# Conv, scan and attention hybrid on one core: B spread by one bf16 product, later sums, and other stages placed by estimates

## The chip, the cores and the metric

The kernel runs on one core of a Trainium2 chip. The metric is device time in microseconds (us) of one execution. The kernel before takes 9288.97 us (median of three runs, 9285.59 to 9299.49). Engines are called as the profile calls them: PE is TensorE (PEld its weight loads), DVE is VectorE, ACT is ScalarE, POOL is GpSimd, SP is SyncE.

## The reference, cut to what matters

Four images of 56 x 56 tokens and 96 channels pass two layers with a selective scan, each in four directions, then two attention and feed-forward layers. The heart is this recurrence over 3136 tokens, for 192 channels with 16 states each:

```python
def step(h, inp):
    da_t, db_t, x_t, c_t = inp
    h = da_t * h + db_t * x_t[..., None]
    y_t = jnp.einsum('bds,bs->bd', h, c_t)
    return (h, y_t)
...
dt = jax.nn.softplus(jnp.einsum('blr,dr->bld', dt_raw, dtw) + dtb)
d_a = jnp.exp(dt[..., None] * a)
d_b = dt[..., None] * b_ssm[:, :, None, :]
```

Two layers, four images and four directions, cut in chunks of 448 tokens, make 224 chunks. A chunk has eight rounds of three scans over 128 lanes: 1792 rounds, 5376 scans.

## The kernel before

One round spreads B over 128 lanes (TensorE, an fp32 product with a selection matrix), multiplies it with dt times u into `v` (VectorE, the third of three products often GpSimd), scans (VectorE, with the decays of ScalarE in PSUM), multiplies with C into `hc` (GpSimd), and sums over the states (TensorE).

```python
def begin(n):
    ch, e, q = rounds[n]
    b = self.spread_b(ch, q)                       # PE: sel x cf, fp32
    v = sp.tile([128, NG, CS + 2], F32, name="v", bufs=3)
    ahead = NQ * e + q not in (OWN_TAIL if ch.l and ch.i else OWN)
    if ahead:                                      # third product on GpSimd
        nc.gpsimd.tensor_tensor(v[:, 2, TOKENS], ch.du[e][:, 2], ch.cb[q][:, 1], ALU.mult)
    return b, v, ahead
...
for n, (ch, e, q) in enumerate(rounds):
    b, v, ahead = nxt
    for g in range(2 if ahead else 3):
        nc.vector.tensor_tensor(v[:, g, TOKENS], ch.du[e][:, g], b, ALU.mult)
    nxt = begin(n + 1)
    self.prepare(ch, nexts.get(ch), r)             # the next chunk's cf, dt, du
    yield "C", n, r                                # gap for other stages
    for g in range(NG):
        if g == 2:
            yield "F", n, r                        # second gap
        nc.vector.tensor_tensor_scan(v[:, g, way], da[g][:, way], v[:, g, way], 0.0, ALU.mult, ALU.add)
        ...
        decay(n + 1, g)                            # ACT: exp into da[g]
        if g == 1:
            carried(n + 1, nxt[1])                 # ACT: carried state into v
    hc = ...                                       # POOL: v times C
    if late is not None:
        self.add_up(*late)                         # PE: sums of round n - 1
    late = (ch, e, q, hc)
```

The other stages (loading, the middle with its convolution, the tails) are generators. At each `yield` of the scans they proceed by one step, thinned by fixed turns:

```python
if slot == "F":
    next(rest, None)
elif (r != 2 or p > 4) and taken * FULL <= TURNS[p] * u:
    taken += 1
    next(rest, None)
...
alone(net.tail(3))                                 # the last image's tail, after the scans
```

A stretch below is one layer and image, 28 chunks. Beside stretch 0 runs the loading, beside 1 to 4 the middles of images 0 to 3, beside 5 to 7 the tails of images 0 to 2.

Of the kernel before, what the change touches and what calls it, by code (L numbers as in the profile page):

```python
# [20 lines left out]
HS = 56  # L21
# [15 lines left out]
NW = 13  # L37
NWIN = 3
OWN = (3, 4, 5)
OWN_TAIL = (4, 5)  # L40

FULL = 4 * NCS * NE * NQ - 13
TURNS = (150, 150, 150, 150, 150, 220, 220, 220)
BANKS = 2
DEPTH = 3
ORDER = ((0, 0), (0, 1), (1, 0), (1, 1))
WD = NE * 128 + C + NE + NE * NQ * NG
# [32 lines left out]
def lay_out(i):  # L80
# [28 lines left out]
    for l, (xw, dw, db, al, dd) in enumerate(scan):  # L109
        r = RANK[l]  # L110
        for k in range(4):
            t = xw[k].T
            m = np.zeros((128, NE, 2, 64), np.float32)
            m[:C, :, 0, :32] = np.concatenate([t[:, r + NS :], t[:, r : r + NS]], 1).reshape(NE, C, 32).swapaxes(0, 1)
            m[:C, :, 0, 32 : 32 + r] = t[:, :r].reshape(NE, C, r).swapaxes(0, 1)
            m[:, :, 1] = m[:, :, 0]
            wt = np.zeros((128, C), np.float32)
            for e in range(NE):
                wt[64 * e + 32 : 64 * e + 32 + r] = dw[k].T[:, C * e : C * e + C]
            bias = np.zeros((128, NE), np.float32)  # L120
            bias[:C] = db[k].reshape(NE, C).T
            a = al[k].reshape(NE, NG, 32, 4, NQ).transpose(3, 2, 0, 4, 1).reshape(128, -1)
            wd[l, k] = np.concatenate([m.reshape(128, -1), wt, bias, a], 1)
        c128.add(f"{l}D", dd.T.reshape(NE, C, 4).swapaxes(0, 1))
# [35 lines left out]
class Net:  # L160
    def __init__(self, ctx, tc, aps, at, out):
# [5 lines left out]
        self.dram = pool("dram", bufs=1, space=bass.MemoryType.DRAM)  # L167
        self.setup()
        self.dg = None
        self.held = self.lend = 0  # L170
        self.U = [self.big.tile([C, L], F32, name=f"U{e}") for e in range(NE)]
        self.Y = [self.big.tile([C, L], F32, name=f"Y{e}") for e in range(NE)]
        self.sp = pool("scan", bufs=2)
        self.wp = pool("work", bufs=2)
        d = lambda name, *shape: [self.dram.tile(list(shape), F32, name=f"{name}{i}") for i in range(NB)]
        self.xd, self.xrd = d("x", C, L), d("xr", C, L)
        self.ud, self.zd, self.yd, self.md = d("u", DI, L), d("z", DI, L), d("y", DI, L), d("m", DI, L)

    def ps(self):
        return self.psum.tile([128, 512], F32, tag="ps", name="ps", bufs=BANKS)  # L180

    def w(self, rows=128):
        return self.wp.tile([128, CW], F32, tag="w", name="w", bufs=NW)[:rows]
# [42 lines left out]
    def setup(self):  # L226
# [17 lines left out]

        self.sel = const.tile([128, NQ, 128], F32, name="sel")
        for q in range(NQ):
            nc.vector.tensor_copy(
                self.sel[:, q].rearrange("p (s d) -> p s d", s=4),
                self.ident[:, NS + q : NS + q + 13 : 4].unsqueeze(2).to_broadcast([128, 4, 32]),
            )  # L250
# [78 lines left out]
        with tc.tile_pool(name="stage", bufs=1) as st:  # L329
            t = st.tile([C, 2, 3, 128], F32, name="q96")  # L330
# [75 lines left out]
    def parameters(self, ch):  # L406

        nc, sp = self.nc, self.sp
        if ch.first:
            for n in range(4):  # L410
                a = slice(n * L // 4, (n + 1) * L // 4)
                for e in range(NE):
                    nc.sync.dma_start(self.U[e][:, a], self.ud[ch.i][C * e : C * e + C, a])
        if ch.step == 0:
# [5 lines left out]
            p.wt = wd[:, a : a + C]  # L420
            a += C
# [4 lines left out]
        ch.par = self.p  # L426

# [19 lines left out]
    def step_size(self, ch, e, ps):  # L447
        rows = slice(64 * e + 32, 64 * e + 32 + RANK[ch.l])
        self.nc.tensor.matmul(ps[:C], ch.par.wt[rows], ch.cf[rows], start=True, stop=True)
# [46 lines left out]
    def prepare(self, ch, follow, r):  # L496
# [9 lines left out]
        elif r == 1:  # L506
            self.step_sizes(follow)
        elif r == 2:
            self.softplus(follow)
        elif r == 3:  # L510
# [13 lines left out]
    def prepare_ahead(self, far, r):  # L524

        if far is not None:
            if r == 5:
                self.parameters(far)
            elif r > 5:
                self.project_step(far, r - 6)  # L530

    def spread_b(self, ch, q):

        ps = self.psum.tile([128, 512], F32, tag="b", name="b", bufs=1)[:, :CS]
        self.nc.tensor.matmul(ps, self.sel[:, q], ch.cf, start=True, stop=True)  # L535
        return ps

    def scans(self):
# [9 lines left out]
        for l in range(2):  # L548
            for i in range(NB):
                for n, (orient, rev) in enumerate(ORDER):  # L550
                    for step in range(NCS):
# [4 lines left out]
                        ch.first = n == 0 and step == 0  # L556
# [7 lines left out]
        self.parameters(first)  # L564
        self.project_step(first, 0)
# [20 lines left out]
        def begin(n):  # L586
# [4 lines left out]
            if ahead:  # L591
                nc.gpsimd.tensor_tensor(v[:, 2, TOKENS], ch.du[e][:, 2], ch.cb[q][:, 1], ALU.mult)  # L592
            return b, v, ahead

        def carried(n, v):
            ch, e, q = rounds[n]
            at = CS + 1 if ch.rev else 0
            if ch.step:
                nc.scalar.copy(v[:, :, at : at + 1], ch.par.carry[:, e, q].unsqueeze(2))  # L599
# [4 lines left out]
        late = None  # L604
        for n, (ch, e, q) in enumerate(rounds):
# [8 lines left out]
            if more:  # L614
                nxt = begin(n + 1)
            self.prepare(ch, nexts.get(ch), r)
            yield "C", n, r
            self.prepare_ahead(afters.get(ch), r)
            if late is not None and late[2] == 0 and n > 1:
                self.keep_sums(*rounds[n - 2])  # L620
            for g in range(NG):
                if g == 2:
                    yield "F", n, r
# [7 lines left out]
                if more:  # L631
                    decay(n + 1, g)
                    if g == 1:
                        carried(n + 1, nxt[1])
            hc = sp.tile([128, NG, CS], F32, name="hc")
            nc.gpsimd.tensor_tensor(hc, v[:, :, TOKENS], ch.cb[q][:, 0].unsqueeze(1).to_broadcast([128, NG, CS]), ALU.mult)  # L636
            if late is not None:
                self.add_up(*late)
            late = (ch, e, q, hc)
        self.add_up(*late)  # L640
# [3 lines left out]
    def add_up(self, ch, e, q, hc):  # L644

        nc = self.nc
        if q == 0:
            self.y = self.psum.tile([128, 512], F32, tag="y", name="y", bufs=1)[:, :CS]

        for n, g in enumerate((0, 1, 2, 2)):  # L650
            nc.tensor.matmul(  # L651
                self.y[32 * n : 32 * n + 32], self.four, hc[:, g], start=q == 0 or n == 3, stop=n == 3,
            )
        if q < NQ - 1:
            return
        o = self.y[:C].rearrange("p (a b) -> p a b", b=HS)
        a, w = (self.U[e], self.skip[ch.l][:, e]) if ch.skip else (self.Y[e], self.ident[:C, :C])
        nc.tensor.matmul(o, w, self.in_order(a, ch.orient, ch.c * CS, CS), start=False, stop=True)  # L658

    def keep_sums(self, ch, e, q):  # L660
# [3 lines left out]
        if ch.last:  # L664
            self.nc.sync.dma_start(self.yd[ch.i][C * e : C * e + C], self.Y[e])
# [17 lines left out]
    def spread_factor(self, eps, *terms):  # L683
# [10 lines left out]
        yield "F0"  # L694
# [3 lines left out]
        yield "C1"  # L698
# [7 lines left out]
    def normed(self, eps, x, held, out=None):  # L706

        xc = self.factor(x)
        yield "F0"
        sq = self.squares(xc)  # L710
        yield "C1"
# [6 lines left out]
    def project(self, l, i, xr, s):  # L718
# [4 lines left out]
        yield "C2"  # L723
# [4 lines left out]
        yield "C1"  # L728
        t = [self.w(), self.w()]
        nc.scalar.activation(t[0], ps[0], AF.Silu, bias=b[:, 1:2])  # L730
        nc.scalar.activation(t[1][64:], ps[1][64:], AF.Silu, bias=b[64:, 2:3])
        nc.scalar.activation(t[1][:64], ps[1][:64], AF.Identity, bias=b[:64, 2:3])
        p = self.ps()[:, :CW]
        nc.tensor.matmul(p, self.in_w[l][:, :128], xr, start=True, stop=True)
        yield "F0"
# [27 lines left out]
    def conv(self, diag, win, lo, *parts):  # L763
# [5 lines left out]
        for n, tap in enumerate(taps):  # L769
# [9 lines left out]
            if n % 2 and n < 8:  # L779
                yield "C1"  # L780
# [10 lines left out]
    def overlap(self, part, n, depth):  # L791

        live, c = [], 0
        while live or c < n:
            if self.slot == "C" and c < n and len(live) < depth:
                live.append([part(c), "C0", 0])
                c += 1
            for g in list(live):
                new = int(g[1][1:])
                if g[1][0] == self.slot and sum(h[2] for h in live) - g[2] + new <= BANKS - self.lend:  # L800
# [3 lines left out]
            self.held = sum(h[2] for h in live)  # L804
            yield


    def load(self, i):
# [3 lines left out]
        def part(c):  # L812
# [4 lines left out]
            yield "C1"  # L817
# [3 lines left out]
            yield "F0"  # L821
            x = self.w(C)
            nc.scalar.copy(x, ps)
            yield "C1"
# [4 lines left out]
        yield from self.overlap(part, NCW, DEPTH)  # L829

    def middle(self, i):
# [5 lines left out]
        def part(c):  # L837
# [8 lines left out]
            yield "C1"  # L846
# [3 lines left out]
            yield "C1"  # L850
# [4 lines left out]
            yield "C0"  # L855
            g.append(self.w())
            nc.scalar.activation(g[0], ps[0], AF.Gelu, bias=self.b1[:, :1])
            yield "C2"
# [3 lines left out]
            yield "C0"  # L862
# [3 lines left out]
            yield "C1"  # L866
# [3 lines left out]
            yield "C1"  # L870
# [5 lines left out]
        yield from self.overlap(part, NCW, DEPTH)  # L876

        if self.dg is None:
            yield from self.run(self.diagonals(par("c128", "1conv_wa"), par("c128", "1conv_wb")[:64]))
            self.dg = self.got  # L880
        dga, dgb = self.dg

        def convolve(c):
# [4 lines left out]
            yield "C1"  # L888
            ps = self.ps()[:, :CW]
            yield from self.conv(dga, wa, lo, (ps, c * CR, CR))  # L890
            yield "C1"
            t = self.w()
            nc.scalar.activation(t, ps, AF.Silu, bias=par("c128", "1conv_ba"))  # L893
            ps = self.ps()
# [3 lines left out]
            yield "C0"  # L898
# [8 lines left out]
        yield from self.overlap(convolve, NCW, 2)  # L907

    def run(self, part):

        def whole(_):
            yield "C1"
            self.got = yield from part

        yield from self.overlap(whole, 1, 1)


    def tail(self, i):
# [3 lines left out]
        if len(self.dg) > 1:  # L922
            yield from self.run(self.diagonals(par("c96", "1dw_w")))
            self.dg = self.got
        (dgx,) = self.dg

        def part(c):
# [5 lines left out]
            yield "C1"  # L933
# [3 lines left out]
            yield "F0"  # L937
            fo = self.w(C)
            nc.scalar.activation(fo, ps, AF.Relu, bias=self.bn1[1], scale=self.bn1[0])
            yield "C1"  # L940
# [4 lines left out]
            yield "F0"  # L945
            nc.scalar.activation(fo, ps, AF.Identity, bias=self.bf)
            yield "C1"
# [3 lines left out]
            yield "F1"  # L951
            sa = self.squares(pa)
            yield "C1"
# [4 lines left out]
            yield "F1"  # L958
            nc.scalar.activation(yb, pb, AF.Square)
            yield "C1"  # L960
            nc.vector.tensor_tensor(zb, zb, pb, ALU.mult)
            f = yield from self.spread_factor(1e-5, (sa, self.avg192), (yb, self.avg192[:64]))
            yield "F0"
            rs = self.w(C)
            nc.scalar.copy(rs, f)
            yield "C1"
# [3 lines left out]
            yield "C1"  # L970
            nc.vector.tensor_tensor(rs, rs, ps, ALU.mult)
            xc = self.factor(fo, rs)
            yield "F0"
            sq = self.squares(xc)
            nc.scalar.activation(fo, xc, AF.Copy, scale=par("c96", "1fus_ln_g"))
            yield "C1"
# [7 lines left out]
            yield "F0"  # L984
            nc.scalar.activation(x, x, AF.Identity, bias=par("c96", "1fus_ln_b"))
            yield "C1"
# [4 lines left out]
        yield from self.overlap(part, NCW, DEPTH)  # L991
        for n in range(2):
            yield from self.run(self.attention(n))
            wq, bq = self.got

            def ffn(c):
# [4 lines left out]
                yield "C1"  # L1001
                ps = self.ps()[:C, :CW]
                nc.tensor.matmul(ps, wq, xr, start=True, stop=True)
                yield "C1"
                nc.vector.scalar_tensor_tensor(x, ps, bq, x, ALU.add, ALU.add)
                xc = self.factor(x)
                yield "F0"
# [3 lines left out]
                yield "C1"  # L1011
                f = yield from self.spread_factor(1e-5, (sq, self.avg96[:, :1]))
                yield "C1"
                xq = self.wp.tile([C, CW], F8, name="xq", bufs=DEPTH)
                nc.vector.tensor_tensor(xq, xs, f, ALU.mult, saturate=False)
                h = self.wp.tile([128, 3, CW], F16, name="h", bufs=2)
                ps = self.ps()[:, :CW]
                nc.tensor.matmul(ps, self.w1q[:, n, 0, :], xq, start=True, stop=True)
                yield "F0"
                nc.scalar.copy(h[:, 0], ps)  # L1020
                nc.scalar.activation(h[:, 0], h[:, 0], AF.Relu, bias=self.b1q[:, n, :1])
                yield "C2"
# [4 lines left out]
                yield "F0"  # L1027
# [3 lines left out]
                yield "C1"  # L1031
                hq = self.wp.tile([128, 3, CW], F8, name="hq", bufs=2)
# [150 lines left out]
```

## Time and profile before

| | before |
|---|---|
| start to first scan | 121 us |
| scans | 8675 us |
| tail after the scans | 507 us |
| busy in the scans: VectorE, GpSimd, TensorE | 7881, 7338, 7172 us |
| VectorE idle in the scans | 8675 - 7881 = 794 us |

The length of a stretch or a round in this document is the distance between the starts of its first scan and of the next one's, in the timeline of VectorE. The prediction shows the views that carry its argument. Two lines of the page that it does not show matter later: the clock granted to TensorE in forty slices (tenths of full speed), and the group of the sums (count, busy us, mean ns of one, idle time before and its releaser).

```profile
PEclk8988899888888888888898889888898889988875
L651 PE MATMUL y<-hc,four 128*32 128x448 f32 x14336 | 1980.0, 628 | 424.5 <-POOL hc L636 396.2
```

The clock stands at eight or nine tenths through the scans.

### The profile page before, as it was taken

To read this page: it belongs to the slowest core of one execution; us is meant where nothing else is said; L and a number is where in the kernel's file an instruction comes from. 1 tells how busy PE (TensorE), PEld (TensorE's weight loads), DVE (VectorE), ACT (ScalarE), POOL (GpSimd) and SP (SyncE) were. 2 spreads that over 40 slices of the span, in tenths; PEclk is the share of its full clock that TensorE was granted. 3 is DMA by queue.
4 is the path that set the end of the run, shared out by engine and by line. 5 is a ranking of instruction groups with operands and counts; after the bars stand their busy time and mean duration, and the time that the engine had idled before them with its cause. 6 is when DMAs were issued, how large, how long until landed. Compare 5 with 4: busy or idle time off the path is not lost.

```text
span 9302.9 us, 112892 instructions
## 1 busy us (share of the span) xinstructions
PE 7648.6 (82%) x30134; PEld 2655.7 (29%) x30134; DVE 7967.6 (86%) x10251; ACT 6080.1 (65%) x12093; POOL 7416.2 (80%) x3872
## 2 busy tenths in 40 slices
PE   7788787787878778887878879888898879988786
PEld 3222122222222222221222223332332223332244
DVE  5999999988998989989898989999889998999711
ACT  5777677666776667666776656666666666666523
POOL 4889888878887888878887888888888888888711
PEclk8988899888888888888898889888898889988875
DMA  5777766656666676667666676656666666666411
GB/s 154 177 177 169 172 169 162 155 138 170 168 157 147 157 172 164 155 148 172 166 162 149 154 180 154 149 148 150 176 152 155 150 154 162 157 154 153 115 33 31
DMA packets 940551, 1415.81 MB, mean 152 GB/s; under 512 B 175042, under 2 KB 926148, under 8 KB 938276
## 3 DMA queue, kind: packets, MB, share of 16 engines
q1 hardware_dynamic: 939136, 1406.79, 62.0%
q8 instruction: 238, 3.90, 0.2%
q14 instruction: 405, 3.32, 0.1%
q10 hardware_dynamic: 772, 1.80, 0.1%
HBM read 1139.85 MB, written 268.14 MB: 151 GB/s over the span
## 4 chain that ended last, share of the span: by engine, by line
PE 31%; DVE 25%; issue 12%; ACT 12%; DMA 10%; POOL 6%; SPq 3%; DVEq 0%; POOLq 0%; ACTq 0%
DVE v L626 17%; DVE v L612 7%; PE b L535 6%; PE y L651 5%; PE ps L775 4%; POOL hc L636 4%; ACT da L584 4%; DMA cb<-cd 3%; PE y L658 3%; PE pp L401 2%; DMA du<-dd 2%; PE ps L693 2%; PE ps L701 1%; SPq L485 1%; ACT L584 1%
## 5 line engine op out<-in xcount | busy, mean ns | idle before, releaser
L636 POOL TENSOR_TENSOR hc<-v,cb 128x1344 f32<-128x1344 f32 x1792 | 5155.8, 2877 | 1033.1 <-DVE v L626 571.3
L626 DVE TENSOR_TENSOR_SCAN v<-da,v 128x449 f32<-128x449 f32 (+1 forms) x5376 | 5469.6, 1071 | 362.8 <-ACT v L599 298.2
L584 ACT ACTIVATE da<-dt,na 128x448 f32<-128x448 f32 x5376 | 3358.5, 634 | 1531.4 <-DVE v L626 1477.4
L535 PE MATMUL b<-cf,sel 128*128 128x448 f32 x3584 | 2062.6, 661 | 804.5 <-DVE v L612 794.2
L612 DVE TENSOR_TENSOR v<-du,b 128x448 f32<-128x448 f32 x4172 | 2332.5, 606 | 297.3 <-PE b L535 275.0
L651 PE MATMUL y<-hc,four 128*32 128x448 f32 x14336 | 1980.0, 628 | 424.5 <-POOL hc L636 396.2
L592 POOL TENSOR_TENSOR v<-du,cb 128x448 f32<-128x448 f32 x1204 | 1378.5, 1145 | 81.1 <-DMA cb<-cd 64.9
L535 PEld LDWEIGHTS b<-cf,sel 128*128 128x128 f32 x3584 | 636.8, 212 | 2406.3 <-DVE v L612 1793.5
L651 PEld LDWEIGHTS y<-hc,four 128*32 128x32 f32 x14336 | 298.6, 114 | 1856.3 <-POOL hc L636 1104.8
L697 POOL TENSOR_TENSOR rs<-rs,power 112x4 f32<-112x4 f32 x252 | 254.3, 1010 | 685.2 <-ACT rs L696 498.5
L663 ACT COPY Y<-y 96x448 f32<-96x448 f32 x448 | 340.7, 761 | 623.8 <-PE y L658 623.0
L401 PE MATMUL pp<-U,wd 96*128 96x448 f32 x896 | 645.0, 807 | 75.1 <-DMA wd<-in_wd_dram 69.8
L775 PE MATMUL ps<-win,dg 64*64 64x220 f32 (+11 forms) x2016 | 567.3, 479 | 31.2 <-ACT w L893 30.7
L468 POOL TENSOR_TENSOR duc<-dtc,U 96x448 f32<-96x448 f32 x448 | 562.7, 1256 | 11.6 <-ACT dtc L462 11.6
L658 PE MATMUL y<-Y,ident 96*96 96x448 f32 x672 | 546.6, 902 | 0.0
L584 ACT ACT_TABLE_LOAD x385 | 494.0, 1283 | 14.4 <-DMA dt<-dd 7.5
L630 ACT COPY carry<-v 128x3 f32<-128x3 f32 x1536 | 293.6, 191 | 127.2 <-DVE v L626 123.9
L693 PEld LDWEIGHTS ps<-avg,w 96*112 96x112 f32 (+1 forms) x2240 | 315.2, 208 | 126.1 <-issue 53.2
L775 PEld LDWEIGHTS ps<-win,dg 64*64 64x64 f32 (+2 forms) x2016 | 249.6, 166 | 324.0 <-issue 255.3
L701 PE MATMUL ps<-ident,rs 112*96 112x112 f32 x2016 | 301.6, 307 | 33.3 <-POOL rs L697 31.1
L701 PEld LDWEIGHTS ps<-ident,rs 112*96 112x96 f32 x2016 | 281.5, 203 | 156.4 <-issue 77.2
L693 PE MATMUL ps<-avg,w 96*112 96x1 f32 (+1 forms) x2240 | 308.5, 255 | 20.0 <-ACT w L680 5.1
(218 smaller groups left out, 5497.3 us busy)
## 6 DMA issues: line engine op xcount, KB each, us to landing
cb<-cd SPq DMA_DIRECT2D x3584, 112.0 KB, 4.0
dt<-dd SPq DMA_DIRECT2D x1792, 168.0 KB, 4.0
du<-dd SPq DMA_DIRECT2D x1792, 168.0 KB, 3.7
dd<-dtc SPq DMA_DIRECT2D x448, 168.0 KB, 2.0
dd<-duc SPq DMA_DIRECT2D x448, 168.0 KB, 2.0
U<-u SPq DMA_DIRECT2D x64, 294.0 KB, 6.9
y<-Y SPq DMA_DIRECT2D x16, 1176.0 KB, 6.7
z<-w SPq DMA_DIRECT2D x56, 224.0 KB, 2.4
```

The costliest lines, as they stand in the source:

```text
L401: self.nc.tensor.matmul(ch.ps.rearrange("p (a b) -> p a b", b=HS), ch.par.wx[:, e], self.in_order(self.U[e], ch.orient, ch.c * CS, CS), st ...
L535: self.nc.tensor.matmul(ps, self.sel[:, q], ch.cf, start=True, stop=True)
L584: nc.scalar.activation(da[g][:, TOKENS], ch.dt[e][:, g], AF.Exp, scale=ch.par.na[:, e, q, g : g + 1])
L592: nc.gpsimd.tensor_tensor(v[:, 2, TOKENS], ch.du[e][:, 2], ch.cb[q][:, 1], ALU.mult)
L612: nc.vector.tensor_tensor(v[:, g, TOKENS], ch.du[e][:, g], b, ALU.mult)
L626: nc.vector.tensor_tensor_scan(v[:, g, way], da[g][:, way], v[:, g, way], 0.0, ALU.mult, ALU.add)
L636: nc.gpsimd.tensor_tensor(hc, v[:, :, TOKENS], ch.cb[q][:, 0].unsqueeze(1).to_broadcast([128, NG, CS]), ALU.mult)
L651: nc.tensor.matmul(self.y[32 * n : 32 * n + 32], self.four, hc[:, g], start=q == 0 or n == 3, stop=n == 3,)
L658: nc.tensor.matmul(o, w, self.in_order(a, ch.orient, ch.c * CS, CS), start=False, stop=True)
L693: nc.tensor.matmul(ps[:NT, q : q + 1], sq[:, b], avg, start=n == 0, stop=n == len(terms) - 1)
L701: nc.tensor.matmul(ps[:, b], rs[:, q : q + 1].to_broadcast([NT, C]), self.ident[:NT, :NT], start=True, stop=True)
L775: self.nc.tensor.matmul(o[:, a - r0 : e - r0, x0:x1], diag[:, tap], win[:, a + dy - lo : e + dy - lo, x0 + dx : x1 + dx], start=n == 0, st ...
```

## The change

The intent: TensorE gets rid of the four passes of fp32 for B, nothing that VectorE waits for stands behind GpSimd or behind other stages, and other stages are placed by what ScalarE and TensorE have to spare. B is kept exact: the projection writes B three times into `cf`, GpSimd subtracts the upper 16 bits once and twice, and one bf16 product adds the three upper halves.

```diff
-        self.nc.tensor.matmul(ps, self.sel[:, q], ch.cf, start=True, stop=True)
+        self.nc.tensor.matmul(ps, self.sel[:, q], self.upper(ch.cf), start=True, stop=True)
+    def upper(self, x):
+        return x.bitcast(BF16).rearrange("p (t h) -> p t h", h=2)[:, :, 1]
+    def split(self, ch, n):
+        x = ch.cf[64 + 32 * n :]
+        self.nc.gpsimd.tensor_tensor(x, x, self.upper(x), ALU.subtract)
...
-OWN = (3, 4, 5)
-OWN_TAIL = (4, 5)
+OWN = (3, 4)
+OWN_TAIL = (3,)
+SPARE = (1.2, 3.0)
+ACT_LIMIT, PE_LIMIT = 4.3, 6.0
...
             more = n + 1 < len(rounds)
             if more:
-                nxt = begin(n + 1)
+                nxt = begin(n + 1)                 # now copies the carried state too
+            if len(late) == 2:
+                ended = late.pop(0)
+                self.add_up(*ended)                # sums of round n - 2, after B
             self.prepare(ch, nexts.get(ch), r)
+            self.half_round()
+            self.spend((0.6, 0, 3.8, 0, 0, 0, 0, 0)[r], ...)
+            self.limit = ACT_LIMIT if r >= SOFTPLUS else 0.5 + 0.95 * 2 * (SOFTPLUS - r)
             yield "C", n, r
...
+    def half_round(self):
+        self.backlog = [max(0.0, a - b) for a, b in zip(self.backlog, SPARE)]
+    def room(self, act, pe):
+        a, p = self.backlog
+        return not self.paced or (act == 0 or a + act <= self.limit) and (pe == 0 or p + pe <= PE_LIMIT)
...
-            yield "C1"
+            yield "C0 a3.2"                        # a step's estimate: 3.2 us of ScalarE
...
+                if p == 7:
+                    lanes.insert(0, chain(net.fuse(3), net.attend(3)))
+    net.late()                                     # eight banks, six pieces in flight
+    alone(lanes)
```

(Cut; the comments on the right are added here.) The second layer's passes are reordered so that the last runs forward by rows, and the fusion of the last image can begin during the scans. Weights of the next pass are fetched three rounds earlier.

## The prediction

> **What bounds the kernel now.** I read first the page's busy shares, then the busy time by stretch, a quiet stretch of the timeline, the waits by engine, and the groups of instructions.
>
> The shares of the span show four engines close together, none full:
>
> ```profile
> span 9302.9 us, 112892 instructions
> PE 7648.6 (82%) x30134; PEld 2655.7 (29%) x30134; DVE 7967.6 (86%) x10251; ACT 6080.1 (65%) x12093; POOL 7416.2 (80%) x3872
> ```
>
> The timeline puts the first scan at 121 us and the last at 8795 us. Between them lie 1792 rounds (224 chunks of eight) with the other stages in their gaps; after them the last tail runs alone. Busy time in the scans, in the tail's fusion and in its two attention and feed-forward layers (columns: stretch, length, busy of PE, PEld, DVE, ACT, POOL, clock granted to TensorE, DMA share, GB/s):
>
> ```profile
> 121.00:8796.00 8675.00, 7171.55 (x28520) 2385.72 (x28520) 7881.41 (x10049) 5900.04 (x11748) 7338.18 (x3790) 0.88 0.66 160
> 8796.00:9034.00 238.00, 209.28 (x749) 108.16 (x745) 25.63 (x48) 45.42 (x92) 31.92 (x29) 0.77 0.13 37
> 9034.00:9303.00 269.00, 185.26 (x622) 114.74 (x622) 40.83 (x71) 90.20 (x182) 35.44 (x35) 0.51 0.10 30
> ```
>
> So the time is 121 + 8675 + 507 us. A quiet round, late in the scans where no other stage is left, shows the bare cycle of VectorE and GpSimd:
>
> ```profile
> 8718.93 1.12 DVE L612 TENSOR_TENSOR v<-du,b 128x448 f32<-128x448 f32 x2
> 8719.15 2.89 POOL L636 TENSOR_TENSOR hc<-v,cb 128x1344 f32<-128x1344 f32 x1
> 8719.97 3.05 DVE L626 TENSOR_TENSOR_SCAN v<-da,v 128x449 f32<-128x449 f32 x3
> 8721.99 1.15 POOL L592 TENSOR_TENSOR v<-du,cb 128x448 f32<-128x448 f32 x1
> 8722.94 1.12 DVE L612 TENSOR_TENSOR v<-du,b 128x448 f32<-128x448 f32 x2
> ```
>
> VectorE has no gap: a round is 4.01 us (8718.93 to 8722.94). Where the third product is VectorE's too, a round takes 4.55 us (8705.83 to 8710.37 in the same view). A chunk with three such rounds is then 5 x 4.01 + 3 x 4.55 = 33.7 us, and undisturbed chunks do take 34. The average is 8675/224 = 38.7 us. The excess is VectorE's idle time of 8675 - 7881 = 794 us plus its own work for other stages. Its waits within the scans, then those of POOL and PE:
>
> ```profile
> DVE v L626 <- ACT v L599: 298.2, 269, 6.7
> DVE v L612 <- PE b L535: 275.0, 185, 11.0
> DVE hq L1033 <- ACT h L1030: 70.1, 42, 4.8
> POOL hc L636 <- DVE v L626: 570.1, 476, 7.7
> POOL hc L636 <- PE y L651: 195.5, 143, 9.6
> PE y L651 <- POOL hc L636: 393.9, 441, 7.2
> ```
>
> The first two are 573 of the 794 us: ScalarE brings the carried state late, since its three-element copy queues behind long functions of other stages, and TensorE brings the spread B late, since B queues behind other products and behind sums that wait for GpSimd. VectorE is the bound with two feeders that are late now and then.
>
> **What the Trainium skill says.** "FP8 and Floating Point Precision", TensorE Precision Notes: a true FP32 product is four passes of the array. The trace agrees in size: one spread of B, two recorded instructions, takes 1.02 us, against a fourth of that for one pass of 448 columns. "GPSIMD Engine Reference", 3.1: about 2.6 cycles an element at 1.2 GHz for two inputs, the same for any number of partitions up to 128. It gives 0.97 us plus dispatch for 448 elements; the trace has 1134 ns at 128 partitions and 1130 ns at 64. "TensorE: Matmul & The Clock Gate", Part 1: after an idle window of 3.4 us the array gets half its clock. The tail's layers at a clock of 0.51 agree. "ScalarE: Activation LUTs", What ACT_TABLE_LOAD costs: 1283 ns and a drain of 1380 ns. The trace shows 1283 ns and no drain (load at 4475.26, function at 4476.56).
>
> **The change part by part.**
>
> ```profile
> L535 PE MATMUL b<-cf,sel 128*128 128x448 f32 x3584 | 2062.6, 661 | 804.5 <-DVE v L612 794.2
> L592 POOL TENSOR_TENSOR v<-du,cb 128x448 f32<-128x448 f32 x1204 | 1378.5, 1145 | 81.1 <-DMA cb<-cd 64.9
> L845 POOL TENSOR_TENSOR w<-w 64x448 f32<-64x448 f32 x28 | 31.6, 1130 | 0.0
> ```
>
> (Columns: group, count, busy us, mean ns, idle before and its releaser.)
>
> 1. *B in one bf16 product.* 1792 spreads fall from 1.02 to about 0.26 us (a fourth): TensorE loses some 1360 us of work, 7172 to about 5810. Off the end's path in itself; it helps by making B late less often.
> 2. *The split into three parts* is new on GpSimd: two subtractions a chunk, of 64 and 32 partitions by 448. Partitions do not shorten them (1130 against 1134 ns), so 448 x 1.13 = **+506 us**.
> 3. *Third products.* The rounds in which VectorE makes it fall by one in each of the 224 chunks. VectorE: 224 x (4.55 - 4.01) = **-121 us**. GpSimd: 224 x 1.145 = **+256 us**.
> 4. *Sums two rounds late, carried state early.* The instruction order shows B's product ahead of the sum in each round now, and the carry copy ahead of other ScalarE work. This attacks the 275 and 298 us. I give it 420 of these 573 us: TensorE still has convolutions, and a ScalarE function with its two table loads (3.2 us) can still delay a decay.
> 5. *Pacing* leaves the work the same (the table loads are counted alike, some 750 in both) and spreads it. It should take the worst chunks (45 to 52 us between scans in the trace) to about 40.
> 6. *The tail.* The last pass of the second layer is now in row order, so fusing the last image starts during the scans. By the instruction order less moves than it seems: after the last sum stand 782 rows of TensorE work against 848; two thirds of the last fusion, a piece of image 2 and both layers of image 3 are left. The gain is from eight PSUM banks for two and six pieces in flight for three. The 394 us of TensorE work ran partly at half clock. At full clock I count some 136 products at 0.97 us, some 170 means and 150 spreads at about 0.24 us, and 50 us of transposes and small ones: about 260 us. With start, serial attention and drain: **300 us**, for 507.
>
> GpSimd within the scans: 7338 + 506 + 256 + 25 (fusion moved in) = **8125 us**. VectorE: 7881 - 121 + 15 = **7775 us**. The bound passes from VectorE to GpSimd. The floor of a chunk rises: 36.2 us for GpSimd (8 x 2.877 + 6 x 1.145 + 2 x 1.256 for dt times U + 2 x 1.13 + 1.6 of others), against some 34.4 us for VectorE before. What is won is the removal of waits.
>
> GpSimd's idle time in the scans was 8675 - 7338 = 1337 us, mostly for want of scans (570 us) and of ScalarE. When it lags, its input lies ready and these shrink. What stays is the image boundaries, where B and C wait on DMA (65 and 43 us), and rounds in which three buffers of v do not bridge the unevenness. I put 305 us: scans 8125 + 305 = 8430. Sum: 121 + 8430 + 300 = **8850 us**, 4.7% less.
>
> **Rivals.**
> - *GpSimd swallows the gain.* If it idles at 6 to 7% because it and VectorE are tied by three v buffers, the scans take 8675 as before, and only the tail gains: about 9095 us. For it: quiet chunks get slower (34 to 36). Against it: VectorE then has 10% of slack, and it was the waits for others that made bad chunks.
> - *VectorE's feeders were all.* If the subtractions are cheaper than I count (one operand is bf16, of which the trace has no example) and GpSimd is nearly gapless, the scans take 8200 and the tail 270: about 8590 us. The moving of still more products to GpSimd speaks for it: a tuner would not do that with GpSimd as the clear bound.
> - *A new wait through the early carry copy.* It needs a v buffer freed by GpSimd, and ScalarE executes in order, so a lagging GpSimd could stall the decays. That gives 8900 to 9050 us.
> - *The tail stays cold*, bound by chains at half clock: 400 us, 100 more than counted.
>
> **Range and chances.** Scans of 8270 to 8580 and a tail of 260 to 380, unlikely to err together: 8650 to 9050 us. Two per cent faster is under 9103 us, which needs nearly the whole rival of a swallowed gain to fail: 0.93 faster, 0.05 within, 0.02 slower.
>
> **What would show it.** Right: GpSimd's share above VectorE's, at 94% or more in the scans; B's group with 1792 instructions and under 700 us; the waits of scan for carry and of product for B down from 573 to about 150 us; some 448 subtractions near 1.13 us; a tail near 300 us with a clock above 0.8. Wrong: VectorE busier than GpSimd, subtractions well off 1.1 us, a new large wait of ScalarE or VectorE for GpSimd, or a tail of 400 us at 0.5.

## The result

The changed kernel takes **9236.03 us** (median of four runs, 9226.99 to 9245.01) against 9288.26 us of the kernel before in the same rounds. Ratios here are those of the record, worked out there from the fast runs of the same rounds; they are not quite the ratio of the medians. This one is 0.9941, with a 95% interval of 0.9924 to 0.9959. That is 0.6% faster, in the class "same", and outside the predicted range. All runs were in the fast state.

Shares of the span and the granted clock, from the page of the changed kernel:

```profile
span 9225.2 us, 109826 instructions
PE 7293.5 (79%) x28342; PEld 2344.9 (25%) x28342; DVE 7916.1 (86%) x10029; ACT 6072.5 (66%) x12091; POOL 8056.3 (87%) x4544
PEclk7767677676777677775778668876787767876776
```

GpSimd is ahead of VectorE, as predicted, but far from full. The clock has dropped to six or seven tenths in most slices. Busy times in the scans and in the tail (length, then PE, PEld, DVE, ACT, POOL, clock, DMA share, GB/s):

```profile
114.00:8887.00 8773.00, 6936.75 (x26885) 2133.46 (x26885) 7831.72 (x9832) 5901.89 (x11753) 7981.01 (x4466) 0.73 0.66 158
8887.00:9225.00 338.00, 283.06 (x1211) 168.99 (x1209) 64.89 (x112) 128.76 (x269) 62.79 (x59) 0.75 0.15 42
```

The tail fell from 507 to 338 us, and the start from 121 to 114 us. But the scans, which were to fall from 8675 to 8430 us, **rose** to 8773. TensorE lost only 7172 - 6937 = 235 us of busy time. The groups say why:

```profile
L699 PE MATMUL y<-hc,four 128*32 128x448 f32 x14336 | 2357.5, 740 | 62.7 <-POOL hc L682 59.5
L562 PE MATMUL b<-cf,sel 128*128 128x448 bf16 x1792 | 799.2, 446 | 1564.1 <-DVE v L649 1560.1
L632 POOL TENSOR_TENSOR v<-du,cb 128x448 f32<-128x448 f32 x1428 | 1632.7, 1143 | 57.2 <-DMA cb<-cd 42.3
L575 POOL TENSOR_TENSOR cf<-cf 64x448 f32<-64x448 f32 x448 | 419.0, 935 | 38.1 <-ACT cf L459 3.0
```

B's group fell from 2062.6 to 799.2 us, but the unchanged sums rose from 1980.0 to 2357.5 us, 628 to 740 ns each. The waits in the scans, of VectorE and then of ScalarE, POOL and PE (in all, times, longest):

```profile
DVE v L674 <- ACT da L624: 335.7, 254, 3.7
DVE v L649 <- PE b L562: 201.8, 104, 4.7
ACT v L635 <- POOL hc L682: 293.7, 366, 3.2
ACT cf L459 <- PE pp L420: 128.5, 54, 7.8
POOL hc L682 <- PE y L699: 174.0, 90, 4.6
PE y L699 <- POOL hc L682: 58.4, 118, 2.2
```

VectorE's wait for the carried state (298 us) has become one for decays (336 us): the copy now runs early, but it waits for GpSimd to free a buffer of v (294 us). The wait for B fell only from 275 to 202 us. TensorE's wait for GpSimd did fall, from 394 to 58 us.

The stretches, in us, for the kernel before, the changed one and three experiments:

| stretch | before | changed | e5 turns of before | e10 TensorE limit only | e17 best |
|---|---|---|---|---|---|
| 0 | 1015 | 1039 | 1026 | 1014 | 1015 |
| 1 | 1085 | 1070 | 1089 | 1063 | 1058 |
| 2 | 1084 | 1081 | 1016 | 1036 | 1025 |
| 3 | 1087 | 1081 | 1028 | 1041 | 1029 |
| 4 | 1075 | 1080 | 1034 | 1056 | 1029 |
| 5 | 1110 | 1139 | 1163 | 1140 | 1140 |
| 6 | 1108 | 1141 | 1150 | 1145 | 1148 |
| 7 | 1110 | 1139 | 1156 | 1124 | 1133 |

### The profile page after: what moved, and what is told of

Its sections match the earlier page's. It is cut to its first block, busy times and chain, and to the rows that moved or that the text cites. A ratio compares the mean times of both kernels' runs of the same rounds, so it can differ in the third digit from the quotient of the medians.

```text
span 9225.2 us, 109826 instructions
## 1 busy us (share of the span) xinstructions
PE 7293.5 (79%) x28342; PEld 2344.9 (25%) x28342; DVE 7916.1 (86%) x10029; ACT 6072.5 (66%) x12091; POOL 8056.3 (87%) x4544
## 5 line engine op out<-in xcount | busy, mean ns | idle before, releaser
L649 DVE TENSOR_TENSOR v<-du,b 128x448 f32<-128x448 f32 x3948 | 2211.1, 605 | 251.0 <-PE b L562 201.8
L699 PE MATMUL y<-hc,four 128*32 128x448 f32 x14336 | 2357.5, 740 | 62.7 <-POOL hc L682 59.5
L562 PE MATMUL b<-cf,sel 128*128 128x448 bf16 x1792 | 799.2, 446 | 1564.1 <-DVE v L649 1560.1
L632 POOL TENSOR_TENSOR v<-du,cb 128x448 f32<-128x448 f32 x1428 | 1632.7, 1143 | 57.2 <-DMA cb<-cd 42.3
L746 POOL TENSOR_TENSOR rs<-rs,power 112x4 f32<-112x4 f32 x252 | 255.2, 1014 | 418.9 <-ACT rs L745 292.4
L825 PE MATMUL ps<-win,dg 64*64 64x220 f32 (+10 forms) x1962 | 611.7, 538 | 0.0
L696 PE MATMUL y<-Y,ident 96*96 96x448 f32 x672 | 580.0, 956 | 20.2 <-ACT carry L678 19.5
L624 ACT ACT_TABLE_LOAD x385 | 494.0, 1283 | 15.7 <-DMA dt<-dd 8.9
L635 ACT COPY v<-carry 128x3 f32<-128x3 f32 x1536 | 285.7, 186 | 296.3 <-POOL hc L682 293.7
L562 PEld LDWEIGHTS <-sel 128*128 128x128 bf16 x1792 | 199.1, 111 | 1083.0 <-issue 1080.6
L575 POOL TENSOR_TENSOR cf<-cf 64x448 f32<-64x448 f32 x448 | 419.0, 935 | 38.1 <-ACT cf L459 3.0
L472 PE MATMUL pp<-cf,wd 12*96 12x448 f32 (+1 forms) x564 | 374.6, 753 | 0.2 <-ACT dtc L485 0.2
```

Source lines behind the costliest of these rows:

```text
L562: self.nc.tensor.matmul(ps, self.sel[:, q], self.upper(ch.cf), start=True, stop=True)
L575: self.nc.gpsimd.tensor_tensor(x, x, self.upper(x), ALU.subtract)
L624: nc.scalar.activation(da[g][:, TOKENS], ch.dt[e][:, g], AF.Exp, scale=ch.par.na[:, e, q, g : g + 1])
L696: nc.tensor.matmul(o, w, self.in_order(a, ch.orient, ch.c * CS, CS), start=True, stop=False)
L699: nc.tensor.matmul(self.y[32 * n : 32 * n + 32], self.four, hc[:, g], start=n == 3, stop=n == 3 or q == NQ - 1,)
L825: self.nc.tensor.matmul(o[:, a - r0 : e - r0, x0:x1], diag[:, tap], win[:, a + dy - lo : e + dy - lo, x0 + dx : x1 + dx], start=n == 0, st ...
```

## The experiments

After the result I had three theories for the scans. **Clock**: with a part of its work gone TensorE is granted less clock, so all its other products come later. **GpSimd**: at 7981 of 8773 us it is the bound. **Placement**: the estimates put other stages where they hurt. Eighteen kernels ran; the ratios of all are against the kernel before in the same rounds (its medians were 9288 to 9304 us).

### e1: B's product four times

```diff
-        self.nc.tensor.matmul(ps, self.sel[:, q], self.upper(ch.cf), start=True, stop=True)
+        for _ in range(4):
+            self.nc.tensor.matmul(ps, self.sel[:, q], self.upper(ch.cf), start=True, stop=True)
```

> The changed kernel with B's bf16 product issued four times over into the same bank (same result, about as much TensorE work as the four passes of before). Clock theory (the change took TensorE so much work that its clock is granted at 0.73 in place of 0.88, so that all its other products got longer and feed VectorE late): the clock rises to 0.80 or more, the sums' group falls from 740 to under 680 ns, and the time falls by 50 to 200 us, to 9030 to 9180 us, though TensorE does more. GpSimd theory (its 91% in the scans is the bound): 9236 us within 20. Plain-work theory (TensorE's queue is the bound): slower by 100 us or more.

9237.2 us, ratio 0.9945. From its page:

```profile
PEclk8888888888888888988888889988898888988887
L700 PE MATMUL y<-hc,four 128*32 128x448 f32 x14336 | 2046.3, 648 | 18.1 <-POOL hc L683 17.0
```

The clock is back (mean 0.863 against 0.734 over the span) and the sums are at 648 ns, by redundant work alone. So the lower clock is real, and it is caused by the smaller load. The time did not move: neither the gain of the clock theory nor the loss of the plain-work theory is seen. But work and clock change together here. VectorE's wait for decays fell from 336 to 297 us and its wait for B rose from 202 to 246 us, so a gain by the one that the other takes back is not excluded. What is shown is that less work at the lower clock and more work at the higher one take the same time.

### e2: B in fp32 again, no subtractions

```diff
-        self.nc.tensor.matmul(ps, self.sel[:, q], self.upper(ch.cf), start=True, stop=True)
+        self.nc.tensor.matmul(ps, self.sel[:, q], ch.cf, start=True, stop=True)
-            self.split(follow, 0)
...
-            self.split(follow, 1)
```

(With the fp32 selection and the weight layout of before.)

> The changed kernel with B as one fp32 product again, without the two GpSimd subtractions, all else kept. Clock theory: clock back to 0.85 or more, as in the run with B four times, and faster than 9236 us by 50 us or more. GpSimd theory: GpSimd loses 419 us of work and the time falls by 150 us or more, well below the run with B four times. If the bf16 product was a gain in itself: slower than 9236 us.

9235.1 us, ratio 0.9946, clock 0.862. GpSimd lost 8056 - 7643 = 413 us of work and the time did not move. Beside the pacing, the whole bf16 part is worth nothing either way. For GpSimd alone the run to compare with is e1: TensorE has about the same work in both (7641 us busy there, 7674 us here) and the same clock, GpSimd has 8073 us there and 7643 us here, and the times are 9237 and 9235 us. So GpSimd's load is not what holds the scans, as long as both limits stand.

### e3: the carried state late again

```diff
-            if ch.step:
-                nc.scalar.copy(v[:, :, at : at + 1], ...)      # in begin(n + 1)
+                    if g == 1:
+                        carried(n + 1, nxt[1])                 # after the second decay
```

> The changed kernel with the carried state copied after the second decay, where it was. Carry theory (the early copy makes ScalarE wait 294 us for GpSimd to free a v buffer, and the decays behind it come late, 336 us of VectorE's waits): the waits for decays fall below 120 us and the time falls by 50 us or more. Rival (the early copy helps and the decays are late for other reasons): VectorE waits for the carry copy again, 200 us or more, and the time is the same or longer.

9298.14 us, ratio 1.0002. VectorE's waits in its scans:

```profile
DVE v L677 <- ACT v L639: 346.9, 233, 4.8
...
DVE v L677 <- ACT da L624: 102.8, 90, 3.6
```

The rival held. Late, the copy and the decays cost 347 + 103 = 450 us of waits; early, the decays cost 336 and the copy nothing. The early copy is a gain of about 60 us, although it adds a wait of ScalarE for GpSimd.

### e4: the third products divided as before

```diff
-OWN = (3, 4)
-OWN_TAIL = (3,)
+OWN = (3, 4, 5)
+OWN_TAIL = (4, 5)
```

> The changed kernel with the third products divided between VectorE and GpSimd as before (three a chunk on VectorE, two in the later tail chunks): GpSimd loses 256 us, VectorE gains 121. GpSimd theory: faster by 50 us or more, most in the last three image stretches. Rival (VectorE and its feeders bind): slower by 50 to 120 us.

9241.39 us, ratio 0.9948: no difference. GpSimd's busy time is 222 us lower, but VectorE's is 63 us higher (7979 for 7916 us), so this run alone would not settle it. It agrees with e1 and e2: GpSimd is not the bound.

### e5: the turns of before instead of the estimates

```diff
-            net.slot, net.lend, net.paced = slot, int(r == 1), True
+            net.slot, net.lend, net.paced = slot, int(r == 1), False
...
+                if slot == "C":
+                    if not ((r != 2 or p > 4) and taken * full <= turns[p] * u):
+                        continue
+                    taken += 1
                 lanes = go_on(lanes)
```

> The changed kernel without the estimates: other stages proceed in every gap in which a bank is free, thinned by the fixed turns of before (fusing in flight limited to three pieces so that it passes the check). Pacing theory (the estimates place the work worse than the fixed turns did and give back in the scans what the tail won): the scans fall from 8770 us by 80 us or more and the time is 9160 us or less. Rival (the scans' excess is a fixed price for each piece of other work, wherever it is placed): 9236 us within 40.

9097.49 us, ratio 0.9797: 1.4% less than the changed kernel. The placement theory holds. The table of stretches shows where: 2 to 4 lose 46 to 65 us each, while 1 and 5 to 7 get longer by 9 to 24 us. (Fusing was limited to three pieces in flight, here and in e7, e9, e10, e12 to e16 and e18; without the limit e5 and e7 deadlocked in the check for want of work buffers. By the code it touches the tail alone, since beside the scans three pieces are the most in any case; the tail of e10 is 350 us against 338.)

### e6: sums one round late

```diff
             if len(late) == 2:
                 ended = late.pop(0)
-                self.add_up(*ended)
...
+            if late:
+                self.add_up(*late[-1])            # at the end of the round, before the next B
             late.append((ch, e, q, hc))
```

> The changed kernel with the sums of a round issued at the end of the next round, before the following spread of B, as before. If the late sums are a gain: VectorE's waits for B rise from 202 us and the time rises by 30 us or more. Rival (they only move TensorE's wait for GpSimd, and delay the buffers of hc instead): 9236 us within 25, with GpSimd's waits for sums, 174 us, falling.

9196.91 us, ratio 0.9910, with runs spread from 9188 to 9241 us: neither expectation. With the sums one round late VectorE's wait for B rose from 202 to 560 us, but the time did not rise. By the medians it is 39 us lower; the intervals of the two ratios overlap (0.9881 to 0.9938 here, 0.9924 to 0.9959 for the changed kernel), so a gain is not shown either. In the trace, which is of the run of 9241 us, the wait for decays fell from 336 to 172 us, and so did other waits of VectorE (step 4 below): waits changed places.

### e7: the last fusion after the scans

```diff
-                if p == 7:
-                    lanes.insert(0, chain(net.fuse(3), net.attend(3)))
     net.late()
-    alone(lanes)
+    alone(lanes + [chain(net.fuse(3), net.attend(3))])
```

> The changed kernel with the fusion of the last image begun only after the scans (three pieces in flight, to pass the check). If the early start is a gain: the tail grows from 338 to 400 us or more, the scans fall by less than half of that, and the time rises by 40 us or more. Rival (what is put beside the scans costs the scans as much): the time within 25 us of 9236.

9315.66 us, ratio 1.0024. The tail is 424 us, and the scans are 8793 us, no shorter. The early start is worth about 80 us, and what it puts into the scans does not lengthen them.

### e8: no change of tables for other stages (wrong result on purpose)

```diff
-AF.Silu ... AF.Gelu
+AF.Identity
```

> A wrong result on purpose: the changed kernel with Silu and Gelu replaced by Identity, which needs no other table (about 160 fewer loads of softplus's neighbours and their returns to the exponential). ScalarE theory (a function with its two loads holds up the decays, and that makes the scans' excess): the waits of scans for decays, 336 us, fall under 200 us, and the time falls by 150 us or more, almost all in the first five image stretches. Rival (TensorE's queue makes the excess): less than 60 us.

9137.27 us, ratio 0.9841; the result is wrong, as intended (relative error 0.2). My count of loads was off: 324 fell away, not 160. Between the two expectations: 1.0% for 395 us of ScalarE work (6073 to 5677). The wait for decays hardly fell (310 us). Long functions are a part of the cost, not all of it.

### e9 and e10: one limit at a time

```diff
-        return not self.paced or (act == 0 or a + act <= self.limit) and (pe == 0 or p + pe <= PE_LIMIT)
+        return not self.paced or act == 0 or a + act <= self.limit        # e9
+        return not self.paced or pe == 0 or p + pe <= PE_LIMIT            # e10
```

> The changed kernel, paced by the ScalarE estimate alone; the TensorE limit is taken away (fusing three pieces deep, as in the run with the turns of before). If the TensorE limit does the harm (it bunches convolutions where the next chunk's projection needs TensorE): 9120 us or less. If the ScalarE limit does it: 9200 us or more. If the fixed thinning of before was what helped in that run, and not the absence of limits: both this and the TensorE-alone run near 9236 us or longer.

> The changed kernel, paced by the TensorE estimate alone; the ScalarE limit is taken away. If the ScalarE limit does the harm (it holds work back in the first two rounds of a chunk and bunches it behind): 9120 us or less. If the TensorE limit does it: 9200 us or more.

e9: 9307.43 us, ratio 1.0016. e10: **9093.29 us, ratio 0.9786**. The ScalarE limit does the harm; taking it away gains 0.9941 - 0.9786, or 1.55% (144 us). Beside it the TensorE limit is a help: e9, which lacks that one, is 0.75% slower than the changed kernel. The scans of e10 and its waits there:

```profile
113.00:8735.00 8622.00, 6898.78 (x26899) 2133.80 (x26899) 7805.90 (x9830) 5900.09 (x11743) 7980.36 (x4465) 0.74 0.67 161
```

```profile
DVE v L674 <- ACT da L624: 228.8, 245, 3.6
DVE v L649 <- PE b L562: 114.4, 104, 4.8
...
ACT cf L459 <- PE pp L420: 69.7, 52, 4.9
```

All engines do nearly the same work as in the changed kernel, at nearly the same clock, in 151 us less. VectorE's waits for decays and B are 107 and 87 us lower, and ScalarE's wait for the next chunk's projection fell from 128 to 70 us. What such a wait looks like can be seen in a convolution of stretch 2 in the changed kernel's timeline:

```profile
2937.39 5.90 PE L825 MATMUL ps<-win,dg 64*64 64x220 f32 x12
...
2943.13 0.36 PE L562 MATMUL b<-cf,sel 128*128 128x448 bf16 x1
...
2943.53 1.15 DVE L649 TENSOR_TENSOR v<-du,b 128x448 f32<-128x448 f32 x2 [3.55 <-PE b L562]
...
2944.44 0.99 ACT L706 COPY Y<-y 96x448 f32<-96x448 f32 x1 [4.78 <-PE y L699]
```

Twelve convolution matmuls stand in front of B; VectorE waits 3.55 us for B, and ScalarE 4.78 us in order for a sum behind it. The place lies in three chunks of the stretch (17 to 19, counted from 0; 2882 to 3025 us) that last 47 to 48 us each, where a quiet chunk lasts 34. VectorE's waits in them account for the difference:

```profile
DVE v L649 <- PE b L562: 31.6, 9, 3.7
DVE v L674 <- ACT da L624: 9.9, 6, 2.6
```

The expectation says that the limit holds work back and bunches it behind. The traces do not show more bunching. Counted between successive products of B, in stretches 2 to 4, 42 rounds have 16 or more convolution matmuls with the limit, and 42 have them without it. The long chunks have 54 of them each; a chunk of e10 with 92 lasts 38 us. In the long chunks 16 and 12 stand in front of the first two products of B; whether that place is what costs, no run tests. So it is shown that the limit costs the 144 us, and not how. The reserve does not do what it is for either: round 2 of a chunk, with softplus, averages 6.18 us over stretches 1 to 4 with it, 5.91 us without the limit, and 5.71 us without the reserve alone (e15; 5.80 before).

### e11: the kernel before with the deeper tail

```diff
-    alone(net.tail(3))
+    net.late()
+    alone(net.tail(3))
```

> The kernel before with only the deeper tail: after the scans eight banks, twenty work buffers and six pieces of the layers in flight (three of the fusion). If the tail's gain is separable: the stretch after the scans falls from 507 to 400 us or less and the time to 9170 to 9220 us. Rival (the tail's gain came from the last fusion's early start and the mixing with image 2): under 50 us gained.

9219.35 us, ratio 0.9916. The tail is 424 us in place of 507: the depth alone brings some 80 us. A first version with six pieces of the fusion deadlocked in the check and was not run.

### e12: turns, then estimates

```diff
-            net.slot, net.lend, net.paced = slot, int(r == 1), True
+            net.slot, net.lend, net.paced = slot, int(r == 1), p > 4
```

(With the turns of e5 for stretches 0 to 4.)

> The fixed turns of before for the first five image stretches and the estimates for the last three, where the paced kernel's stretches were shorter by 10 to 24 us each than those with turns. If the stretches add up: 9040 to 9080 us, the best so far. If a stretch's length depends on what ran before it: 9097 us or longer.

9070.98 us, ratio 0.9754. Stretches add up.

### e13 and e14: B and the sums once the ScalarE limit is gone

Both are e10 with one part undone: e13 with the edit of e2, e14 with that of e6.

> The kernel paced by TensorE alone, with B as one fp32 product again and no subtractions on GpSimd. If the bf16 product is a gain that the limit hid: slower than 9093 us by 30 us or more. If the bf16 product pays with clock and GpSimd work what it saves: 9093 us within 30. If it is a loss: faster by 30 us or more, with the clock near 0.86.

> The kernel paced by TensorE alone, with the sums one round late, ahead of B, as before. If the late sums keep B off GpSimd's path: VectorE's waits for B rise from 114 us to 300 us or more and the time rises by 30 us or more. If they cost as beside the limit, where one round late was 39 us faster: 9060 us or less.

e13: 9133.71 us, ratio 0.9824, clock 0.87. With e10's 0.9786 the bf16 product is a gain of 0.38%, about 35 us, in spite of the lower clock; the two intervals just touch. Beside the limit the same edit made no difference (e2). e14: 9128.98 us, ratio 0.9814, 0.28% more than e10, with the waits in its scans led by

```profile
DVE v L649 <- PE b L562: 494.2, 409, 5.4
```

against 114 us. The late sums do keep B off GpSimd's path; but with the sums one round late the wait for decays fell again, from 229 to 114 us. The gain of about 26 us by late sums is at the edge of the intervals, and in e6, where nothing is clear of the noise either, the sign is the opposite.

### e15 and e16: which part of the ScalarE limit

```diff
-            self.limit = ACT_LIMIT if r >= SOFTPLUS else 0.5 + 0.95 * 2 * (SOFTPLUS - r)
+            self.limit = ACT_LIMIT                                        # e15
-                    if r < SOFTPLUS:
-                        self.limit -= 0.95
...
-SPARE = (1.2, 3.0)
+SPARE = (2.4, 3.0)                                                        # e16
```

> Both limits, but the ScalarE limit the same in all rounds, without the part that empties ScalarE ahead of softplus (fusing three pieces deep). If the reserve does the harm: 9120 us or less. If the slow drain or the limit itself does it: 9200 us or more.

> Both limits with the reserve kept, but ScalarE's backlog taken to drain at 2.4 us in a half round in place of 1.2 (fusing three pieces deep). If the drain estimate is what is wrong: 9120 us or less. If it is the reserve: 9200 us or more.

e15: 9136.87 us, ratio 0.9823. e16: 9160.3 us, ratio 0.9848. Neither expectation is met cleanly: each half loosened brings back more than half (1.2% and 0.9% of 1.55%). The limit is too tight altogether; it is not one wrong constant.

### e17: the best schedule of each stretch

```diff
-        return not self.paced or (act == 0 or a + act <= self.limit) and (pe == 0 or p + pe <= PE_LIMIT)
+        return not self.paced or pe == 0 or p + pe <= PE_LIMIT
...
-            net.slot, net.lend, net.paced = slot, int(r == 1), True
+            net.slot, net.lend, net.paced = slot, int(r == 1), p not in (2, 3, 4)
```

(With the turns of e5 in stretches 2 to 4 alone. The expectation takes these three stretches from e12's trace and the others from e10's.)

> The turns of before in image stretches 2 to 4 (1024, 1024 and 1040 us there) and TensorE's limit alone in the others (1014, 1063, 1140, 1145, 1124 us), fusing as deep as the change has it. If stretches add up: scans of 8574 us, and with 113 before and 340 after about 9030 us. If they depend on what ran before: 9070 us or more.

**9022.25 us, ratio 0.9703** (0.9689 to 0.9718), correct: 3.0% faster than before, and the best of all. Its scans and tail:

```profile
114.00:8693.00 8579.00, 6880.85 (x26894) 2125.41 (x26893) 7807.97 (x9832) 5899.94 (x11747) 7978.94 (x4463) 0.74 0.68 162
8693.00:9020.00 327.00, 272.15 (x1209) 164.75 (x1201) 64.76 (x114) 130.88 (x274) 64.79 (x61) 0.77 0.17 46
```

### e18: third products as before, without the ScalarE limit

This is e10 with the edit of e4.

> The kernel paced by TensorE alone, with the third products divided between VectorE and GpSimd as before. If moving them to GpSimd is a gain that the limit hid: slower than 9093 us by 30 us or more. If GpSimd at 91% or more is now the bound: faster by 30 us or more. If the two balance: within 30.

9099.51 us, ratio 0.9781 against 0.9786: the two balance, as the third expectation has it. Whether GpSimd, at 7980 of 8622 us in e10, is the bound there is not settled by this: the run gives VectorE the work that it takes off GpSimd, as e13 gives it to TensorE.

## Why the prediction was wrong

**The sum.** It had 121 + 8430 + 300. Measured: 114 + 8773 + 338. The scans alone are 343 us off. The term of the sum that failed is GpSimd's idle time: 8125 busy + 305 idle were predicted, 7981 busy + 792 idle measured. Without the ScalarE limit (e10) the scans are 8622 us: of the 343 us, 151 are the limit's (step 5), and 192 us stay without it (step 4).

**Step 5, pacing**, is the step whose failure an experiment shows. The prediction said that it leaves the work the same and takes the worst chunks to about 40 us. The first half is right, the second wrong: chunks of 47 to 48 us, single before, come three in a row in stretches 2 to 4, and the longest chunk is 50.1 us, against 51.5 before. Taking the ScalarE limit out gives 144 us back (e10), taking all estimates out 1.4% (e5).

**Step 4, waits removed**, was over-credited. It gave 420 of 573 us back. The waits of scan for carry and decay and of product for B were 298 + 40 + 275 = 613 us; they are 336 + 202 = 538 us in the changed kernel, and 229 + 114 = 343 us without the limit. So even there 270 us came back and not 420. The mechanism was right in parts: the early carry copy gains 60 us (e3), and late sums free B from GpSimd (e14). But waits that go come back elsewhere. VectorE in the scans, in us, summed over the list of its waits:

| | before | changed | e10 | e6 sums one round late |
|---|---|---|---|---|
| idle in all (length - busy) | 794 | 941 | 816 | 938 |
| its scans and products, waiting for ScalarE | 338 | 341 | 234 | 174 |
| its scans and products, waiting for TensorE | 275 | 202 | 114 | 560 |
| its work for other stages, waiting for TensorE | 44 | 210 | 238 | 66 |

VectorE's idle time did not fall, not even without the limit. With the sums two rounds late it waits less for B, and longer for the products of other stages; with the sums one round late it is the other way round, at the same idle time. So the 420 us were credited to two named waits, and the time was not theirs alone. This is read from the traces; no run isolates it.

**Step 1, B.** 1792 instructions, as predicted; the group lost 2063 - 799 = 1263 us against 1360. A product takes 446 ns in the mean and 357 ns at least, not a fourth of 1.02 us; the one-pass fp8 products of 448 columns in the kernel before (349 ns at least) could have told this. That TensorE as a whole lost 235 us only, because its clock fell, was not foreseen: its other work takes 6494 us in the changed kernel, against 5586 us before and 5675 us in e1, where the clock is back. Load and clock together did not decide the time (e1). The part's value is nothing beside the limit and about 35 us without.

**Step 2, the split.** 448 subtractions at 935 ns, 419 us in place of 506: mis-sized by a sixth, and without effect on the time (e2).

**Step 3, third products.** GpSimd's group grew by 1632.7 - 1378.5 = 254 us against 256. VectorE's busy time is 7832 us against 7775. The effect is nil (e4, e18).

**Step 6, the tail**, held in size: 338 us against 300, inside its range, though at a clock of 0.75 and not above 0.8. Of the 169 us gained, the depth is about half (e11, some 80 us); the other half is the early fusion (e7, about 80 us), from which the prediction expected little.

**The bound.** "The bound passes from VectorE to GpSimd" was wrong for the changed kernel. A higher busy share is not a bound: some 430 us of GpSimd work, with TensorE's load alike, made no difference (e1 against e2). Without the ScalarE limit this is not tested apart. By the waits, the scans are held by in-order queues that now and then bring B, a decay or a projection late, and neither engine's total shows this. Of the rivals, the third named a real wait (ScalarE for GpSimd's v buffer, 294 us), but e3 shows that it is the lesser evil; the first came nearest in time (9095 us for 9236), but by GpSimd's hold on the scans, which e1 and e2 speak against.

**What stays open.** Stretches 5 and 6 are about 30 us longer than before in nearly all versions with the change. The fp32 B (e13) and the last fusion (e7) do not explain it; with the third products back beside e10 (e18) they are 1128 and 1140 us, and with sums one round late (e14) 1128 and 1132 us, a part of it at most. And I have no run that shows how the ScalarE limit costs its 144 us, or why VectorE's waits in its work for other stages grew.

## What to carry to other kernels

When engines are tied by in-order queues, test a placement rule alone before trusting it: here one limit of a scheduler ate some seven tenths (1.55 of 2.14%) of what a change with several good parts had won. Taking work off an engine, without giving it to another, tells whether it is the bound; its share of busy time does not. Undo each part again after the dominant fault is out, since its worth can differ then (B's product, and perhaps the later sums). And before a removed wait is counted as a gain, add up the engine's idle time: waits change places.

## What the Trainium skill lacked or had wrong

- "TensorE: Matmul & The Clock Gate", Part 1, says that the clock is set by how busy TensorE has been recently, and tells of idle windows that halve it. It gives no measure for a busy stream with gaps. Here a part of the work taken away lowered the mean granted clock in the scans from 0.88 to 0.73, with unchanged sums going from 628 to 740 ns; a bf16 product issued four times over brought it back to 0.863 over the span and 648 ns, at no cost in time. In the packed traces the clock is either full or half: half for 2480 us of the kernel before, and for 4913 us of the changed one.
- "GPSIMD Engine Reference", 3.1, gives one rate for two inputs. With one of them the upper halves of fp32 words read as bf16, 448 elements took 935 ns (in place, at 64 and 32 partitions), against 1134 ns with both fp32.
- "ScalarE: Activation LUTs", What ACT_TABLE_LOAD costs, adds a drain of 1380 ns to each load. In this case's traces the load is 1283 ns and the function follows at once.
